# Two 16-wide attentions of a four-layer kernel: order of the first loads, place of the row statistics, and VectorE work ordered behind the maxima

## The chip, the cores and the metric

The kernel runs on one core of a Trainium2 chip. Its time is the device time of one execution in microseconds (us), the median of several runs. Engines are named as in the profile: PE (TensorE, with PEld for its weight loads), DVE (VectorE), ACT (ScalarE), POOL (GpSimd), SP (SyncE, which issues nearly all DMA transfers here). SBUF is the on-chip memory, PSUM the memory with eight banks that TensorE writes into.

## The reference

x has 16 batches of 256 rows and 256 columns, all float32, and ctx has the same shape. Four layers follow one another, each `x = x + attention(layernorm(x), ctx, ctx)` and `x = x + ffn(layernorm(x))`. The change is in the attentions of layers 0 and 3, which both have 16 heads that are 16 wide:

```
q = xn @ Wq.T (+ bq);  k = ctx @ Wk.T (+ bk);  v = ctx @ Wv.T (+ bv)     # split into 16 heads of 16
attn = softmax(q k^T / 4, over the 256 context rows)
x = x + (attn v, heads joined) @ Wo.T (+ bo)
```

Layer 0 has the biases, layer 3 has none (and shares keys and values in a way that its packed weights take care of). The feed-forward of layer 0 is quantized: the weights are rounded to -1, 0, 1 after a division by their mean absolute value, and the rows of x to 8 bits by their largest absolute value. Layers 1 and 2 are an mLSTM and a 64-wide attention with feed-forwards of their own; layer 3 ends with a mixture of eight experts.

## The kernel before

x stays in SBUF for the whole kernel, one tile per batch (128 partitions x 2 row tiles x 256). `SPECS` says in which order the pieces of a weight pack lie, and `load_pack` issues one transfer for each piece in that order. At the start SP issues the 16 tiles of x, then the eight pieces of `w_l0a`, the three of `w_l0f` (1 MB each), and then the first contexts (`cT`). VectorE computes each batch's row statistics (`batch_stats`: per row tile a BATCH_NORM_STATS2 and a BATCH_NORM_AGGREGATE) as x arrives, and `inv_std` takes all 32 inverse standard deviations at once, by a square root on ACT and a reciprocal on VectorE. That root needs another activation table than the exponentials, so a table is loaded after it.

`narrow_attention` is called by layer 0 (L559) and layer 3 (L1602). It walks over halves: a batch has 16 heads in four quads, and a quad has two halves of two heads. Half i belongs to batch b = i // 8, h = i % 8. Two passes over the scores run at once, and the second is 7 halves later (`LAG`):

- the first pass makes scores with queries on the partitions (`s_ps`, three PSUM banks); VectorE takes their row maxima (`maxima`, L319, two instructions per half, into `top`). After two quads the maxima are turned by TensorE (`top_rows`, `top_ps`) and added into a spare row of q, so that the second pass yields scores minus maximum;
- the second pass makes the scores again with keys on the partitions (`t_ps`, two banks); ACT takes the exponential (`exps`, L347); `weigh` multiplies them with the values (`acc_ps`, one bank, L359), whose extra column of ones yields the sum of the softmax.

The matmuls of both passes alternate within a half (L444): s, t, s, t for the first row tile, and the same for the second.

Around these, each half has other steps for the batches before and after it. All of them use the same two PSUM banks, called "misc", in turn: in h0 `context` (the load of cT of the next batch) and `enter` (normalize), h1 `turn` (`xnT_ps`, copied by ACT to xT) and `top_rows`, h2 `project` q (`qk_ps`), h3 `rest_of` q, h4 `project` k, h5 `rest_of` k and `top_rows`, h7 `values` (`v_ps`). `project` makes a projection on TensorE and lets ACT read it once for the even heads; `rest_of` (L281) is two VectorE instructions that read the same bank again for the odd heads. For an older batch: h2 and h5 `divide` (`o_ps`, L377: four transposes, then VectorE's division), h3 and h7 `back` (`oT_ps`, copied by ACT to oT), h6 `leave` (`out_ps`, the addition to x, the statistics for the next norm, and in layer 0 `left`: four reductions for the rows' largest and smallest value, `l0top`, L536, and every fourth batch the quantization steps).

A caller can add steps by `beside`. In layer 0 it takes one step of the `weights` generator per half from batch 1 on: twelve reductions of the feed-forward weights (`l0tot`, L500), then their rounding. In layer 3 it holds steps of the quantized feed-forward of layer 2, which ends beside the attention: `down` in h3 (`d_ps`, L1510), `steps_of`, `roots` (inverse deviations by `rsqrt`: logarithm and exponential on ACT, five instructions on POOL), the normed output and the experts' gate.

The order of the instructions on an engine is that in which the program issues them, changed by a scheduler of the language, which can move an instruction ahead of others that it doesn't depend on; `tc.issue_after(x)` keeps all that is issued under it behind x. In the built program before, the twelve `l0tot` reductions stand ahead of the first half. `rest_of` k stands ahead of the maxima of h5 and `rest_of` q ahead of those of h3, and the `l0top` reductions ahead of the maxima of h7 and h0.

Of the kernel before, what the change touches and what calls it, by code (L numbers as in the profile page):

```python
# [9 lines left out]
F32 = mybir.dt.float32  # L10
BF16 = mybir.dt.bfloat16
I32 = mybir.dt.int32
AF = mybir.ActivationFunctionType
# [4 lines left out]
P = 128  # L18
# [7 lines left out]

SPECS = {
    "w_l0a": [
        ("wq", 128, (2, 256)), ("wk", 128, (2, 256)), ("bq", 128, (2,)), ("bk", 128, (2,)),
        ("wv", 128, (2, 256)), ("bv", 128, (256,)), ("wo", 128, (2, 256)), ("bo", 128, (256,)),  # L30
    ],
    "w_l0f": [("wg", 128, (2, 1024)), ("wu", 128, (2, 1024)), ("wd", 128, (8, 256))],
    "w_l1a": [("gk", 128, (6, 8)), ("gb", 128, (8,)), ("os", 128, (256,))],
# [24 lines left out]
def kernel(ctx: ExitStack, tc: tile.TileContext, a: dict, out: bass.AP):  # L58
# [19 lines left out]
    nc.gpsimd.memset(eps6, 1e-6)  # L78

    X = [xp.tile([P, 2, D], F32, name=f"x{b}") for b in range(B)]  # L80
    for b in range(B):
        nc.sync.dma_start(X[b], x_v[b])

    def pool(stack, name, bufs, space=None):
        kw = {} if space is None else {"space": space}
# [29 lines left out]
        for t in range(2):  # L115
            tile_stats(mv, 2 * b + t, X[b][:, t, :])

    root = []

    def inv_std(mv):  # L120
        r = stat.tile([P, NT], F32, tag="rstd", name="rstd")
        root[:] = [nc.scalar.activation(r, mv[:, :, 1], AF.Sqrt, bias=eps5)]
        nc.vector.reciprocal(r, r)
        return r

    def normalize(dst, src, mv, r, i):
        nc.vector.tensor_scalar(dst, src, mv[:, i, 0:1], r[:, i : i + 1], ALU.subtract, ALU.mult)

# [8 lines left out]
                nc.tensor.transpose(pt[:, c, t * P : (t + 1) * P], xn[:, t, c * P : (c + 1) * P], ident)  # L137
        nc.scalar.copy(dst[:, :, dst_off : dst_off + S], pt)

    mv = new_stats()  # L140
    for b in range(B):
        batch_stats(mv, b)

    def bcast_max(col, wk, ps):

        t1 = ps.tile([1, P], F32, tag="misc", name="gm_ps")
# [7 lines left out]
        return m  # L154


    def narrow_attention(tag, w, mv, q_bias=None, k_bias=None, v_bias=None, add_bias=None,
                         new=None, rstd=None, wk=None, ps=None, before=None, between=None, beside=None, left=None, one_set=False):

        SCALE = 0.25
        with ExitStack() as st:
            one = pool(st, f"{tag}one", 1)
            if rstd is None:
                new = new_stats()
                rstd = inv_std(mv)
                if one_set:
                    with tc.issue_after(root[0].ins):
                        tables = nc.scalar.preload_act_table_set("natural_log_exp_and_others")  # L170
                    st.enter_context(tc.issue_after(tables.ins))
                wk = pool(st, f"{tag}wk", 2)
                ps = pool(st, f"{tag}ps", 2, PSUM)


            i32 = ident.rearrange("p (a b) -> p a b", b=32)
# [29 lines left out]
                nc.gpsimd.memset(t, 0.0)  # L206
            for t in vals:
                nc.gpsimd.memset(t[:, :, :, 16:17], 1.0)
            if v_bias is not None:

                bT = one.tile([P, 2, P], F32, name="bT")
                pb = ps.tile([P, 2, P], F32, tag="misc", name="bT_ps")
                for c in range(2):
                    nc.tensor.transpose(pb[:, c, :], v_bias[:, c * P : (c + 1) * P], ident)
                nc.vector.tensor_copy(bT, pb)
                pb = ps.tile([P, D], F32, tag="misc", name="bo_ps")
                for c in range(2):
                    nc.tensor.matmul(pb, lhsT=bT[:, c, :], rhs=w["wo"][:, c, :], start=(c == 0), stop=(c == 1))
                nc.vector.tensor_tensor(add_bias, pb, add_bias, ALU.add)

            state = {}

            def context(b):
                cT = wk.tile([P, 2, S], F32, tag="cT", name="cT", bufs=3)
                nc.sync.dma_start(cT, ctxT_v[b])
                state[b] = dict(cT=cT, v=vals[b % 3])

            def enter(b):

                xn = wk.tile([P, 2, D], F32, tag="xn", name="xn", bufs=3)  # L230
                for t in range(2):
                    normalize(xn[:, t, :], X[b][:, t, :], mv, rstd, 2 * b + t)
                if add_bias is not None:
                    for t in range(2):
                        nc.gpsimd.tensor_tensor(X[b][:, t, :], X[b][:, t, :], add_bias, ALU.add)
                state[b]["xn"] = xn

            def turn(b):
                s = state[b]
# [42 lines left out]

            def values(b):
                s = state[b]
                pv = ps.tile([P, 2, D], F32, tag="misc", name="v_ps")
                for t in range(2):
                    for c in range(2):
                        nc.tensor.matmul(  # L288
                            pv[:, t, :],
                            lhsT=s["cT"][:, c, t * P : (t + 1) * P],  # L290
                            rhs=w["wv"][:, c, :],
                            start=(c == 0),
                            stop=(c == 1),
                        )
# [19 lines left out]
            def maxima(n, made):  # L314
                par = n % 2
                top = tops[(n // 2) % 2]
                for j, sp, _ in made:
                    col = 32 * j + 16 - 16 * par
                    nc.vector.tensor_reduce(top[:, :, col], sp, AX.X, ALU.max)  # L319

            def top_rows(m):

# [77 lines left out]
            def leave(b):  # L400
                s = state.pop(b)
                po = ps.tile([P, 2, D], F32, tag="misc", name="out_ps")
                for t in range(2):
                    for c in range(2):
                        nc.tensor.matmul(  # L405
                            po[:, t, :],
                            lhsT=s["oT"][:, c, t * P : (t + 1) * P],
                            rhs=w["wo"][:, c, :],
                            start=(c == 0),
                            stop=(c == 1),  # L410
                        )
                nc.vector.tensor_tensor(X[b], po, X[b], ALU.add)
                batch_stats(new, b)
                if left is not None:
                    left(b, new)

            context(0)
            values(0)
            project(0, "k")
            rest_of(0, "k")  # L420
# [3 lines left out]
            turn(0)  # L424
            project(0, "q")
            rest_of(0, "q")
            if between is not None:
                between()

            LAG = 7  # L430
            halves = 8 * B
            for i in range(halves + (16 if beside is None else 40)):
                b, h = divmod(i, 8)
# [10 lines left out]
                        nc.tensor.matmul(out_, lhsT=l_, rhs=r_, start=True, stop=True)  # L444
                if made:
                    maxima(i // 2, made)
                if h == 5 and b + 1 < B:
                    rest_of(b + 1, "k")
                if flipped:
                    exps((i - LAG) // 2, flipped)  # L450
                if h % 4 == 1 and 5 <= i <= halves + 1:
# [4 lines left out]
                if b + 1 < B:  # L456
                    if h == 0:
                        context(b + 1)
                        enter(b + 1)
                    elif h == 1:  # L460
                        turn(b + 1)
                    elif h == 2:
                        project(b + 1, "q")
                    elif h == 3:
                        rest_of(b + 1, "q")
                    elif h == 4:
                        project(b + 1, "k")
                    elif h == 7:
                        values(b + 1)
# [12 lines left out]
        return new  # L482


    def l0_attn(mv, w, w_f, qp, load):
# [8 lines left out]

        def weights(ps):

            tot = qp.tile([P, 3, 4], F32, name="l0tot")
            for j, n in enumerate(names):
                for c in range(4):
# [24 lines left out]
        def beside(b, h, ps):  # L524
            if not made:
                made.append(weights(ps))
            if h == 4 and 8 <= b < 11:
                load(("w_l1a", "w_l1f", "w_l2a")[b - 8])
            if b >= 1:
                next(made[0], None)  # L530

        def left(b, new):

            for t in range(2):
                for j, op in enumerate((ALU.max, ALU.min)):
                    nc.vector.tensor_reduce(q["top"][:, 2 * b + t, j : j + 1], X[b][:, t, :], AX.X, op)  # L536
            if b % 4 < 3:
                return
            sl = slice(2 * b - 6, 2 * b + 2)
            mean = new[:, sl, 0]  # L540
            r = qp.tile([P, 8], F32, name=f"l0r{b}")
# [14 lines left out]

        with ExitStack() as st:
            sp = pool(st, "l0sp", 2)
            mv = narrow_attention(  # L559
                "l0a", w, mv, q_bias=w["bq"], k_bias=w["bk"], v_bias=w["bv"], add_bias=w["bo"], beside=beside, left=left,  # L560
                one_set=True,
            )
            for _ in made[0]:
                pass
        return mv, q
# [1372 lines left out]
    with ExitStack() as st:  # L1938
        keep = pool(st, "l3keep", 1)
        dram = pool(st, "l3dram", 1, bass.MemoryType.DRAM)  # L1940
        with ExitStack() as s2:
            qp = pool(s2, "l2fq", 1)
            with ExitStack() as s1:
                pw, packs = pool(s1, "l12w", 1), {}
                with ExitStack() as s0:
                    pq, pf, pa = pool(s0, "l0fq", 1), pool(s0, "l0fw", 1), pool(s0, "l0aw", 1)
                    wa = load_pack(pa, "w_l0a")
                    wf = load_pack(pf, "w_l0f")
                    mv, q0 = l0_attn(mv, wa, wf, pq, lambda n: packs.update({n: load_pack(pw, n, lambda z: not late(z))}))
# [116 lines left out]
```

## Time and profile before

| | |
|---|---|
| time of three runs | 3077.2, 3075.54, 3073.31 us, median 3075.54 |
| profiled execution | 3080.25 us, span 3078.5 us |
| layer 0's attention | first scores at 38.69 us, first turned batch after that (`xnT_ps`) at 67.8, then 91.7, 125.8, 152.7, 178.2; from there about 25.8 us a batch, up to 410.9 |
| layer 3's attention | about 2005 to 2452 us, 27.6 us a batch |
| mean granted TensorE clock | 0.951 |

Times in the profile are microseconds from the span's start. A timeline row is start, length, engine, line, operation, output<-input, shapes, how many instructions in a row, and in brackets the engine's idle time ahead of it with what ended that. Rows of the windows have the busy time of each engine in a stretch, with the number of instructions.

### The profile page before, as it was taken

The page shows a single profiled execution, that of the slowest core. Times are in us where ns is not written, and L with a number is a line of the kernel's source. Part 1 is how long each engine was busy: PE and PEld are TensorE (multiplying, and loading weights), DVE is VectorE, ACT ScalarE, POOL GpSimd, SP SyncE. Part 2 cuts the span into 40 slices and gives each one's busy share as a digit, 9 for nine tenths or more (in the row PEclk, how much of TensorE's full clock was granted, in tenths as well). Part 3 has the DMA queues.
Part 4 walks back from the last instruction along what each step waited for, and adds up shares of the span by engine and source line. Part 5 has one row for each costly group of instructions (what it writes and reads, how often), then busy time and mean ns, then how long its engine had stood idle before and what let it go on. Part 6 is the DMA issues. An engine that isn't in the chain of part 4 may idle for free.

```text
span 3078.5 us, 49357 instructions
## 1 busy us (share of the span) xinstructions
PE 2797.2 (91%) x18663; PEld 1990.1 (65%) x18683; DVE 1746.3 (57%) x4397; ACT 1256.5 (41%) x3267; POOL 966.1 (31%) x1929
## 2 busy tenths in 40 slices
PE   6999997778899999999999998698999959999996
PEld 4566664445666666666666665265666648888885
DVE  6777667944555555555555565987777661222221
ACT  2455556623444444444444444634555531111110
POOL 1100003334444444344433333311110034455552
PEclk9999999967999999999999999889999979999998
DMA  5000000010000000000000000411110035676774
GB/s 180 12 12 12 8 1 1 1 48 11 11 11 11 11 11 11 11 11 11 11 11 4 13 18 29 154 45 59 32 32 29 22 110 166 204 222 205 217 211 119
DMA packets 81771, 177.09 MB, mean 58 GB/s; under 512 B 25935, under 2 KB 50526, under 8 KB 70590
## 3 DMA queue, kind: packets, MB, share of 16 engines
q0 software_dynamic: 24864, 105.69, 11.4%
q1 hardware_dynamic: 56670, 68.25, 7.1%
q8 instruction: 147, 2.41, 0.3%
q14 instruction: 90, 0.74, 0.1%
HBM read 147.04 MB, written 31.06 MB: 58 GB/s over the span
## 4 chain that ended last, share of the span: by engine, by line
PE 73%; DVE 12%; POOL 5%; ACT 4%; issue 4%; DMA 1%; POOLq 0%; SPq 0%; DVEq 0%; ACTq 0%
PE h_ps L1857 8%; PE o_ps L1879 8%; PE s_ps L444 7%; PE qk_ps L1031 5%; PE acc_ps L359 4%; PE qk_ps L259 4%; PE acc_ps L1170 4%; PE out_ps L1091 4%; PE s_ps L1112 3%; PE eT_ps L1154 3%; PE v_ps L1047 2%; PE t_ps L444 2%; PE v_ps L288 2%; PE out_ps L405 2%; DVE low L1121 1%
## 5 line engine op out<-in xcount | busy, mean ns | idle before, releaser
L347 ACT ACTIVATE e<-t_ps 128x512 f32<-128x512 f32 x512 | 278.0, 594 | 229.4 <-PE t_ps L444 208.0
L319 DVE TENSOR_REDUCE top<-s_ps 128x2 f32<-128x512 f32 x512 | 330.9, 682 | 51.1 <-PE t_ps L444 44.5
L1131 ACT ACTIVATE e<-s_ps,low 128x256 f32<-128x256 f32 x512 | 236.2, 472 | 286.7 <-DVE low L1121 286.2
L444 PE MATMUL t_ps<-q,k 32*128 32x256 f32 x2048 | 336.2, 409 | 2.7 <-ACT e L347 2.6
L444 PE MATMUL s_ps<-k,q 32*128 32x256 f32 x2048 | 330.9, 411 | 8.4 <-DVE top L319 8.2
L1142 POOL TENSOR_SCALAR e<-e,total 128x256 f32<-128x256 f32 x512 | 238.5, 485 | 310.5 <-DVE total L1139 222.1
L1857 PE MATMUL h_ps<-xgT,w 128*128 128x256 f32 (+1 forms) x1248 | 254.6, 362 | 0.0
L1879 PE MATMUL o_ps<-w,h 128*128 128x256 f32 x1136 | 251.6, 379 | 0.0
L444 PEld LDWEIGHTS s_ps<-k,q 32*128 32x128 f32 x2048 | 197.3, 187 | 80.2 <-issue 35.4
L1857 PEld LDWEIGHTS h_ps<-xgT,w 128*128 128x128 f32 x1248 | 222.1, 192 | 27.6 <-ACT xgT L1846 0.2
L1121 DVE TENSOR_REDUCE low<-s_ps 128x2 f32<-128x512 f32 x256 | 164.3, 683 | 128.6 <-PE s_ps L1112 128.6
L1879 PEld LDWEIGHTS o_ps<-w,h 128*128 128x128 f32 x1136 | 212.9, 190 | 27.4
L444 PEld LDWEIGHTS t_ps<-q,k 32*128 32x128 f32 x2048 | 205.6, 187 | 20.3 <-ACT e L347 14.0
L1869 ACT ACTIVATE h<-h_ps,w 128x256 f32<-128x256 f32 (+1 forms) x156 | 62.5, 451 | 371.0 <-PE h_ps L1857 361.8
L1170 PE MATMUL acc_ps<-eT,v 128*64 128x256 f32 x1024 | 172.6, 397 | 42.3 <-DVE eT L1157 42.1
L1157 DVE COPY eT<-eT_ps 128x512 f32<-128x512 f32 x256 | 165.4, 678 | 21.2 <-PE eT_ps L1154 20.7
L1867 DVE TENSOR_SCALAR h<-h_ps,w 128x256 f32<-128x256 f32 (+1 forms) x156 | 64.6, 455 | 179.1 <-PE h_ps L1857 121.6
L1889 DVE TENSOR_TENSOR y<-o_ps,w 128x256 f32<-128x256 f32 x71 | 27.1, 420 | 226.3 <-PE o_ps L1879 226.3
L1170 PEld LDWEIGHTS acc_ps<-eT,v 128*64 128x64 f32 x1024 | 70.9, 136 | 128.3 <-DVE eT L1157 71.5
L1112 PE MATMUL s_ps<-k,q 64*128 64x256 f32 x1024 | 146.9, 403 | 0.1
L1154 PE MATMUL eT_ps<-ident,e 128*128 128x128 f32 x1024 | 143.9, 286 | 0.0
L359 PE MATMUL acc_ps<-e,vals 128*32 128x256 f32 x2048 | 142.6, 391 | 0.0
(476 smaller groups left out, 5579.3 us busy)
## 6 DMA issues: line engine op xcount, KB each, us to landing
cT<-in_ctxT_dram SPq DMA_DIRECT2D x32, 256.0 KB, 2.8
away<-h SPq DMA_DIRECT2D x30, 256.0 KB, 2.0
h<-away SPq DMA_DIRECT2D x30, 256.0 KB, 4.2
x<-in_x_dram SPq DMA_DIRECT2D x16, 256.0 KB, 5.9
w_l2a<-in_w_l2a_dram SPq DMA_DIRECT2D x4, 1024.0 KB, 6.5
c2T<-in_ctxT_dram SPq DMA_DIRECT2D x16, 256.0 KB, 2.7
c1T<-in_ctxT_dram SPq DMA_DIRECT2D x16, 256.0 KB, 2.7
va<-in_ctx_dram SPq DMA_DIRECT2D x32, 128.0 KB, 2.9
```

The lines of the kernel that those rows point to most:

```text
L319: nc.vector.tensor_reduce(top[:, :, col], sp, AX.X, ALU.max)
L347: nc.scalar.activation(e, tp, AF.Exp)
L359: nc.tensor.matmul(acc[32 * j : 32 * j + 32, par, :], lhsT=s["v"][:, k, 4 * g + j, 16 * par : 16 * par + 32], rhs=es[j][:, k, :], start=(k ...
L444: nc.tensor.matmul(out_, lhsT=l_, rhs=r_, start=True, stop=True)
L1112: nc.tensor.matmul(sp[j][:, t, :], lhsT=q[rows, g % 2, t * P : (t + 1) * P], rhs=k[rows, g % 2, :], start=True, stop=True,)
L1121: nc.vector.tensor_reduce(low[:, :, j], sp[j], AX.X, ALU.max, negate=True)
L1131: nc.scalar.activation(es[j][:, t, :], sp[j][:, t, :], AF.Exp, bias=low[:, t, j : j + 1], accum_out=total[:, t, j : j + 1])
L1142: nc.gpsimd.tensor_scalar(es[j][:, t, :], es[j][:, t, :], total[:, t, j : j + 1], 1.0, ALU.mult, ALU.mult)
L1154: nc.tensor.transpose(pt[:, k, t * P : (t + 1) * P], es[j][:, t, k * P : (k + 1) * P], ident)
L1170: nc.tensor.matmul(s["acc"][64 * j : 64 * j + 64, g % 2, :], lhsT=s["v"][g // 4][:, k, (2 * (g % 4) + j) * 64 : (2 * (g % 4) + j + 1) * 64 ...
L1857: nc.tensor.matmul(pp[:, f - f0, cols_], lhsT=w1[:, c * 1024 + f * P : c * 1024 + (f + 1) * P], rhs=xT[:, c, cols_], start=(c == 0), stop= ...
L1879: nc.tensor.matmul(pp[:, j, :], lhsT=h[:, f, j * P : (j + 1) * P], rhs=w2[:, f * D : (f + 1) * D], start=(f == 0), stop=(f == 7),)
```

## The change

- `w_l0a` is packed in another order: wv, wk, bk, wq, bq, bv, wo, bo. SP's queue starts with x of batch 0, cT of batch 0, these eight pieces, then x of batches 1 to 15 and the next cT. `w_l0f` is loaded by the `weights` generator, whose first step is taken in h7 of batch 0.
- `inv_std` is gone. `roots` uses `rsqrt` (logarithm and exponential) in five pieces: batches 0, 1, 2 to 3, 4 to 9 and 10 to 15. Only the statistics of batches 0 and 1 are computed before the first half; those of batch i + 2 are issued in half i.
- The fold of the value bias into the output bias (`bT`, `bo_ps`) comes after the projections of batch 0.
- `rest_of` k (h5), `rest_of` q (h3), those statistics and roots, and the `l0top` reductions and steps of layer 0 are issued under `tc.issue_after` of the half's last maximum. The reductions are put on a list (`due`) from which each half takes one entry.

In the built program after, VectorE has the two maxima of h3 ahead of `rest_of` q, the two of h5 ahead of `rest_of` k, and the `l0top` reductions two by two behind the maxima of h7 and h0; `l0tot` stands within halves 5 to 11. TensorE has the first three score matmuls of h6 (s, t, s) ahead of the four `o_ps` transposes of h5. In layer 3 `d_ps` has the bank that `oT_ps` had just before, and not that of `qk_ps`.

```diff
 SPECS = {
     "w_l0a": [
-        ("wq", 128, (2, 256)), ("wk", 128, (2, 256)), ("bq", 128, (2,)), ("bk", 128, (2,)),
-        ("wv", 128, (2, 256)), ("bv", 128, (256,)), ("wo", 128, (2, 256)), ("bo", 128, (256,)),
+        ("wv", 128, (2, 256)), ("wk", 128, (2, 256)), ("bk", 128, (2,)), ("wq", 128, (2, 256)), ("bq", 128, (2,)),
+        ("bv", 128, (256,)), ("wo", 128, (2, 256)), ("bo", 128, (256,)),
...
-    for b in range(B):
+
+    def load_x(b):
         nc.sync.dma_start(X[b], x_v[b])
+
+    load_x(0)
...
-    def inv_std(mv):
-        r = stat.tile([P, NT], F32, tag="rstd", name="rstd")
-        root[:] = [nc.scalar.activation(r, mv[:, :, 1], AF.Sqrt, bias=eps5)]
-        nc.vector.reciprocal(r, r)
-        return r
...
-    mv = new_stats()
-    for b in range(B):
-        batch_stats(mv, b)
...
+            def roots(lo, hi):
+                cols = slice(2 * lo, 2 * hi)
+                rsqrt(wk, rstd[:, cols], mv[:, cols, 1], ALU.add, 1.0, 1e-5)
+
+            context(0)
+            if fresh:
+                w = w()
+                q_bias, k_bias, v_bias, add_bias = (w[n] for n in ("bq", "bk", "bv", "bo"))
+                for b in range(1, B):
+                    load_x(b)
+                batch_stats(mv, 0)
+                roots(0, 1)
...
-                    nc.vector.tensor_reduce(top[:, :, col], sp, AX.X, ALU.max)
+                    last_max[:] = [nc.vector.tensor_reduce(top[:, :, col], sp, AX.X, ALU.max)]
...
                 batch_stats(new, b)
                 if left is not None:
-                    left(b, new)
-
-            context(0)
+                    due.extend(left(b, new))
+
             values(0)
...
+            biased(0)
+            if fresh:
+                batch_stats(mv, 1)
+                roots(1, 2)
...
-                if h == 5 and b + 1 < B:
-                    rest_of(b + 1, "k")
+
+                with tc.issue_after(last_max[0].ins):
+                    if h == 5 and b + 1 < B:
+                        rest_of(b + 1, "k")
+                    if h == 3 and b + 1 < B:
+                        rest_of(b + 1, "q")
+                    if fresh and i + 2 < B:
+                        batch_stats(mv, i + 2)
+                        for lo, hi in ((2, 4), (4, 10), (10, B)):
+                            if i + 3 == hi:
+                                roots(lo, hi)
+                    if due:
+                        due.pop(0)()
...
-                    elif h == 3:
-                        rest_of(b + 1, "q")
...
         def weights(ps):
 
+            w_f.update(load("w_l0f"))
+            yield
             tot = qp.tile([P, 3, 4], F32, name="l0tot")
...
-            if b >= 1:
+            if b >= 1 or h == 7:
                 next(made[0], None)
 
         def left(b, new):
 
-            for t in range(2):
+            def extremes(t):
                 for j, op in enumerate((ALU.max, ALU.min)):
                     nc.vector.tensor_reduce(q["top"][:, 2 * b + t, j : j + 1], X[b][:, t, :], AX.X, op)
-            if b % 4 < 3:
-                return
+
+            more = [lambda: extremes(0), lambda: extremes(1)]
+            return more + [lambda: steps(b, new)] if b % 4 == 3 else more
```

More of the change, by code (lines that the diff above doesn't have):

```diff
@@ L116, in batch_stats @@
             tile_stats(mv, 2 * b + t, X[b][:, t, :])
-    root = []
-    def inv_std(mv):
-        r = stat.tile([P, NT], F32, tag="rstd", name="rstd")
-        root[:] = [nc.scalar.activation(r, mv[:, :, 1], AF.Sqrt, bias=eps5)]
-        nc.vector.reciprocal(r, r)
-        return r
     def normalize(dst, src, mv, r, i):
@@ L154, in bcast_max, with narrow_attention @@
         return m
-    def narrow_attention(tag, w, mv, q_bias=None, k_bias=None, v_bias=None, add_bias=None,
-                         new=None, rstd=None, wk=None, ps=None, before=None, between=None, beside=None, left=None, one_set=False):
+    def narrow_attention(tag, w, mv, new=None, rstd=None, wk=None, ps=None, before=None, between=None, beside=None, left=None):
         SCALE = 0.25
@@ L164, in narrow_attention, with context @@
             one = pool(st, f"{tag}one", 1)
[L165 to L171, printed above, removed]
+            q_bias = k_bias = v_bias = add_bias = None
+            fresh, state = rstd is None, {}
+            if fresh:
+                new, mv = new_stats(), new_stats()
+                rstd = stat.tile([P, NT], F32, tag="rstd", name="rstd")
+                tables = nc.scalar.preload_act_table_set("natural_log_exp_and_others")
+                st.enter_context(tc.issue_after(tables.ins))
                 wk = pool(st, f"{tag}wk", 2)
                 ps = pool(st, f"{tag}ps", 2, PSUM)
+            def context(b):
+                cT = wk.tile([P, 2, S], F32, tag="cT", name="cT", bufs=3)
+                nc.sync.dma_start(cT, ctxT_v[b])
+                state[b] = dict(cT=cT)
+            def roots(lo, hi):
[9 more added lines that the diff above has]
+                roots(0, 1)
             i32 = ident.rearrange("p (a b) -> p a b", b=32)
@@ L208, in narrow_attention @@
                 nc.gpsimd.memset(t[:, :, :, 16:17], 1.0)
[L209 to L226, printed above, removed]
             def enter(b):
@@ L232, in enter, with biased @@
                     normalize(xn[:, t, :], X[b][:, t, :], mv, rstd, 2 * b + t)
+                if b:
+                    biased(b)
+                state[b]["xn"] = xn
+            def biased(b):
                 if add_bias is not None:
@@ L235, in enter @@
                         nc.gpsimd.tensor_tensor(X[b][:, t, :], X[b][:, t, :], add_bias, ALU.add)
-                state[b]["xn"] = xn
             def turn(b):
@@ L284, in values @@
                 s = state[b]
+                s["v"] = vals[b % 3]
                 pv = ps.tile([P, 2, D], F32, tag="misc", name="v_ps")
@@ L426, in narrow_attention @@
             rest_of(0, "q")
+            if v_bias is not None:
+                bT = one.tile([P, 2, P], F32, name="bT")
+                pb = ps.tile([P, 2, P], F32, tag="misc", name="bT_ps")
+                for c in range(2):
+                    nc.tensor.transpose(pb[:, c, :], v_bias[:, c * P : (c + 1) * P], ident)
+                nc.vector.tensor_copy(bT, pb)
+                pb = ps.tile([P, D], F32, tag="misc", name="bo_ps")
+                for c in range(2):
+                    nc.tensor.matmul(pb, lhsT=bT[:, c, :], rhs=w["wo"][:, c, :], start=(c == 0), stop=(c == 1))
+                nc.vector.tensor_tensor(add_bias, pb, add_bias, ALU.add)
+            biased(0)
+            if fresh:
+                batch_stats(mv, 1)
+                roots(1, 2)
             if between is not None:
@@ L430, in narrow_attention @@
             LAG = 7
+            last_max, due = [], []
             halves = 8 * B
@@ L482, in narrow_attention, with l0_attn @@
         return new
-    def l0_attn(mv, w, w_f, qp, load):
+    def l0_attn(w, w_f, qp, load):
         q = dict(
@@ L528, in beside, with steps @@
                 load(("w_l1a", "w_l1f", "w_l2a")[b - 8])
-            if b >= 1:
+            if b >= 1 or h == 7:
                 next(made[0], None)
         def left(b, new):
-            for t in range(2):
+            def extremes(t):
                 for j, op in enumerate((ALU.max, ALU.min)):
                     nc.vector.tensor_reduce(q["top"][:, 2 * b + t, j : j + 1], X[b][:, t, :], AX.X, op)
-            if b % 4 < 3:
-                return
+            more = [lambda: extremes(0), lambda: extremes(1)]
+            return more + [lambda: steps(b, new)] if b % 4 == 3 else more
+        def steps(b, new):
             sl = slice(2 * b - 6, 2 * b + 2)
@@ L558, in l0_attn @@
             sp = pool(st, "l0sp", 2)
[L559 to L562, printed above, removed]
+            mv = narrow_attention("l0a", w, None, beside=beside, left=left)
             for _ in made[0]:
@@ L1946, with load @@
                     pq, pf, pa = pool(s0, "l0fq", 1), pool(s0, "l0fw", 1), pool(s0, "l0aw", 1)
-                    wa = load_pack(pa, "w_l0a")
-                    wf = load_pack(pf, "w_l0f")
-                    mv, q0 = l0_attn(mv, wa, wf, pq, lambda n: packs.update({n: load_pack(pw, n, lambda z: not late(z))}))
+                    def load(n):
+                        if n == "w_l0f":
+                            return load_pack(pf, n)
+                        packs[n] = load_pack(pw, n, lambda z: not late(z))
+                    mv, q0 = l0_attn(lambda: load_pack(pa, "w_l0a"), {}, pq, load)
                     mv = l0_ffn(q0)
```

## The prediction

> **What bounds the kernel now.** I read the page's busy shares first, then the windows of the two 16-wide attentions, the groups of L319 and L444, the chain and the timeline of the start, and last the timeline of one batch in each attention.
>
> ```profile
> PE 2797.2 (91%) x18663; PEld 1990.1 (65%) x18683; DVE 1746.3 (57%) x4397; ACT 1256.5 (41%) x3267; POOL 966.1 (31%) x1929
> L319 DVE TENSOR_REDUCE top<-s_ps 128x2 f32<-128x512 f32 x512 | 330.9, 682 | 51.1 <-PE t_ps L444 44.5
> L444 PE MATMUL s_ps<-k,q 32*128 32x256 f32 x2048 | 330.9, 411 | 8.4 <-DVE top L319 8.2
> ```
> ```profile
> 40.00:68.00 28.00, 25.45 (x124) 16.91 (x124) 15.05 (x27) 5.90 (x12) 0.52 (x1) 0.76 0.23 89
> 68.00:92.00 24.00, 22.75 (x235) 14.68 (x236) 14.95 (x31) 13.59 (x30) 1.52 (x2) 1.00 0.05 13
> 92.00:126.00 34.00, 28.57 (x243) 17.95 (x244) 29.12 (x71) 14.03 (x30) 9.85 (x14) 0.89 0.03 9
> 153.00:410.00 257.00, 250.01 (x2432) 166.56 (x2434) 180.88 (x434) 137.74 (x295) 19.62 (x52) 1.00 0.04 10
> ```
> The windows' columns are stretch, length, then busy time of PE, PEld, DVE, ACT and POOL, granted clock, DMA share, GB/s. In layer 0's steady stretch (153 to 410) TensorE is busy 97%, so a wait that opens in its queue adds to the time, and a wait that closes can give back at most the 7 us that are left there. VectorE is 30% idle, and the 8.2 us that score matmuls wait for maxima in the whole kernel cap what earlier maxima can bring directly. Where VectorE is nearly full (92 to 126) the batch takes 34 us, not 25.8.
>
> The start, from the timeline:
> ```profile
> 0.80 9.87 SPq L82 DMA_DIRECT2D x<-in_x_dram  x16
> 11.07 5.58 SPq L97 DMA_DIRECT2D w_l0a<-in_w_l0a_dram  x8
> 17.00 1.50 SPq L97 DMA_DIRECT2D w_l0f<-in_w_l0f_dram  x3
> 18.55 1.68 SPq L225 DMA_DIRECT2D cT<-in_ctxT_dram  x3
> 24.65 7.20 DVE L500 TENSOR_REDUCE l0tot<-w_l0f 128x1 f32<-128x512 f32 x12
> 28.66 3.75 PE L288 MATMUL v_ps<-w_l0a,cT 128*128 128x256 f32 x8 [4.39 <-issue]
> 38.69 1.16 PE L444 MATMUL s_ps<-k,q 32*128 32x256 f32 x12 [0.22 <-ACT q L271]
> ```
> The first context, cT, is the 28th transfer issued, and v_ps starts only at 28.66. One half h5 of layer 0, then one h3 of layer 3:
> ```profile
> 242.90 0.99 DVE L281 TENSOR_SCALAR k<-qk_ps,mask,kadd 128x256 f32<-128x256 f32 x2 [3.10 <-ACT k L271]
> 243.81 1.28 DVE L319 TENSOR_REDUCE top<-s_ps 128x2 f32<-128x512 f32 x2
> 243.94 0.66 PE L377 MATMUL o_ps<-ident,o 128*128 128x128 f32 x4 [0.70 <-DVE k L281]
> 245.00 0.86 DVE L329 SCALAR_TENSOR_TENSOR q<-top_ps,spare,q 128x256 f32<-128x256 f32 x2
> 245.61 1.07 PE L359 MATMUL acc_ps<-e,vals 128*32 128x256 f32 x16
> ...
> 250.51 1.04 DVE L536 TENSOR_REDUCE l0top<-x 128x1 f32<-128x256 f32 x3
> ```
> ```profile
> 2251.99 1.80 PE L1510 MATMUL d_ps<-l2d,hq 128*128 128x256 bf16 x12 [0.29 <-DVE q L281]
> 2252.43 0.38 ACT L398 COPY oT<-oT_ps 128x256 f32<-128x256 f32 x1
> ```
> The o_ps transposes use the PSUM bank that held qk_ps of k, so they wait for VectorE's second read of it, and o_ps stands in TensorE's queue ahead of later scores.
>
> **The change, part by part**, against the profiled execution: 3080.25 us, span 3078.5, 0.15% above the median 3075.54. Negative is faster.
>
> *A, the start: -20.* The order becomes x0, cT, eight pieces of w_l0a (wv first), x1 to x15, cT, w_l0f. wv is then the third transfer; of the x tiles the second landed at 6.6 and the third's statistics ran at 7.36, so v_ps starts near 7.4. From v_ps to the first score took 38.69 - 28.66 = 10.03. Two short ACT steps for the inverse roots now stand ahead of the xT copy (about 0.5, by the 0.38 copy), and the bias fold (bo_ps, 2.08 for four matmuls at 22.20) comes between, about 1.0 of it uncovered: 18.9. The other path is x1, whose statistics VectorE runs before xn of batch 0: eleventh of SP's queue, issued near 7.4 at the x tiles' 0.6 us apart, landing after 2.9 (x0) to 5.9 (the page's median), then 0.75 of statistics, 0.73 of xn, 1.5 to 2 of turning and 4.4 from projecting q: 17.6 to 20.6 with the first steps partly beside it. Gain 18 to 22. POOL's new root steps stand ahead of its 2.6 us of memsets (1.52 to 4.1), which nothing needs before v_ps ends. w_l0f moves behind x15 and cT; its first reader comes in half 5 or later, and the cT behind it only a batch later: zero, and a late reduction would hold up VectorE's queue (rival 2).
>
> *B, VectorE work carried into batches 0 and 1: +4.* Statistics of 14 batches at 0.78 (two tiles at 0.39 from start to start) are 10.9, the twelve w_l0f reductions at 0.60 are 7.2: 18.1 us against the 22.0 that VectorE was idle in 40 to 92 (52.0 - 15.05 - 14.95). They fit, but unevenly. Nothing is one end; 8.5 for one batch that becomes as long as 92 to 126 is the other; I take 4, as neither window is yet full. The extra root steps on ACT (10 for 2) and POOL (25 more) lie beside PE: 0, and at most 1.7 with no cover (ten short steps at the 0.17 of mv, L112).
>
> *C, layer 0: +10.4.* The second read of k moves behind the two maxima of h5. Score matmuls of h5 start at T = 241.73. Where nothing stands ahead, maxima follow scores by 1.16 (scores 254.27, maximum 255.43): 242.89; the read comes 1.19 later (243.81 to 245.00) at 244.08, and o_ps 1.04 after it (242.90 to 243.94): 245.12 instead of 243.94. In the changed program's order three score matmuls of h6 (s, t, s) are issued ahead of o_ps, so they cover part of the wait; a t and the four of the second round are left. With o_ps 0.59 and, at worst, a whole half's 1.08 for these five, acc_ps starts at 246.76 against 245.61: +1.15, in 14 batches +16.1. If the five need only half the time, +0.6 each, +8.4. The other way, the four l0top reductions leave the front of h7's and h0's maxima: h0's scores took 1.52 (251.75 to 253.27) where a clean half takes 1.08; in the 13 batches that have both, 13 x -0.44 = -5.7 (0 if another wait is next: h4, at 262.53, takes 2.02 behind ACT). Moving the read of q behind h3's maxima delays no TensorE step of layer 0: oT_ps there is in the other bank. 16.1 - 5.7 = 10.4.
>
> *D, layer 3: +27.6.* Its o_ps waits in the same way. From the end of qk_ps of k (2257.72) to acc_ps took 3.73; by C's 5.03 from the start of h5 it is +1.3, x14 = 18.2; +0.75 each by C's lower case. In h3, d_ps now shares its bank with oT_ps and waits for the ACT copy, which ended at 2252.81, where d_ps started at 2251.99. Two score matmuls of h4 pass ahead, the other half-round and 1.07 follow d_ps: h4's scores end 4.38 after h3 instead of 3.53: +0.85, in 11 batches +9.4 (0 if they cover it all).
>
> Sum: -20 + 4 + 10.4 + 27.6 = +22.0, so 3102 for an execution like the profiled one, 3097.5 against the median. Ends: A -22, B 0, C 8.4 - 5.7 = 2.7, D 10.5 + 0 = 10.5 give -8.8 (3067); A -18, B 8.5 + 1.7, C 16.1, D 27.6 give +36 (3111).
>
> [...] In 44 to 64 TensorE was busy 3.0 to 4.0 of every 4 us, yet the granted clock was 0.68, 0.75, 0.82, 0.60, 0.54, and eight projection matmuls took 3.56 (60.45) against 1.99 warm (239.81). [...] I go by the row: the low clock comes along.
>
> **Rivals.**
> 1. *The other side: the waits stay covered.* If score matmuls that are issued ahead fill the later o_ps and d_ps, as the 7 us of total TensorE idle in 257 suggests that such gaps get filled, C and D keep only the gain: -20 + 4 - 5.7 = -21.7, 3054. It decides from 21.7 us over 39 waits (14 + 14 + 11): below 0.56 us each the change is no slower. Against it: o_ps already waits 0.70 with its reader first in VectorE's queue.
> 2. *VectorE fills in batches 0 and 1.* Were both to lengthen by 8.5 as batch 2 did, because w_l0f lands late or statistics wait for x behind maxima: B = 17, sum +35, 3110. For it, the row 92 to 126; against it, 22.0 of idle for 18.1.
> 3. *Only layer 0 shows it.* If the steps beside layer 3's attention leave TensorE spare (347 of 363 busy, 16 us idle in 13 batches), D is 0: -20 + 4 + 10.4 = -5.6, 3070.
>
> **How the numbers follow.** Chances: forecast 0.62, rival 1 0.10, rival 2 0.16, rival 3 0.12. The likeliest's own range is 3086 to 3108; the range 3066 to 3112 takes in rivals 2 and 3 and the ends of the sum, and leaves out rival 1 and the tails. About 0.2% (6 us) is what a measurement can tell from no change: faster by more (below 3069), rival 1 and nearly half of rival 3, 0.15; within (to 3082), the rest of rival 3 and the forecast's low tail, 0.10; slower 0.75.
>
> **What would show it.** A: the first s_ps near 19, not 38.7. B: batches 0 and 1 (first score to the third xnT_ps) near 57, not 53. C: VectorE's maxima of h5 ahead of k's read, o_ps idle on DVE k above 1, scores to acc_ps 5.0 instead of 3.88, h0's scores at 1.08, batch period 26.5 instead of 25.8. D: d_ps waiting for ACT oT, period 29.7 instead of 27.6. The prediction is wrong if o_ps waits no longer than 0.7, or if the earlier maxima free s_ps for halves that I counted as filled.

## The result and the profile after

The changed kernel takes 3116.72 us (median of four executions, 3109.18 to 3118.08) against 3076.37 for the kernel before: ratio 1.0126, 95% interval 1.0112 to 1.0141. In a later comparison (e1 below) it was 3108.21, ratio 1.0109 (1.0092 to 1.0126). Its eight executions lie in two groups, near 3108 and near 3117, and both profiled ones are of the lower group, so that the profiles show some 30 us of the loss, and where the other 8 lie is not seen. The forecast was 3097.5, within 3066 to 3112: the first median lies 5 us above that range, the second inside it.

The chain of the start first, in the timeline of the changed kernel:

```profile
6.37 3.75 PE L282 MATMUL v_ps<-w_l0a,cT 128*128 128x256 f32 x8 [6.37 <-DMA w_l0a<-in_w_l0a_dram]
14.16 1.99 PE L252 MATMUL qk_ps<-xT,w_l0a 128*128 128x256 f32 x8 [1.47 <-ACT xT L239]
16.80 0.69 PE L453 MATMUL s_ps<-k,q 32*128 32x256 f32 x2 [0.44 <-ACT q L264]
```

v_ps starts at 6.37 instead of 28.66, and the first scores at 16.80 instead of 38.69: 21.9 us gained. Next, the half h5 of layer 0, and h3 of layer 3, in the places that the prediction showed:

```profile
238.64 0.99 DVE L274 TENSOR_SCALAR k<-qk_ps,mask,kadd 128x256 f32<-128x256 f32 x2
239.54 0.86 DVE L323 SCALAR_TENSOR_TENSOR q<-top_ps,spare,q 128x256 f32<-128x256 f32 x2
239.68 0.66 PE L371 MATMUL o_ps<-ident,o 128*128 128x128 f32 x4 [0.80 <-DVE k L274]
241.32 1.07 PE L353 MATMUL acc_ps<-e,vals 128*32 128x256 f32 x16
```
```profile
2231.36 0.38 ACT L392 COPY oT<-oT_ps 128x256 f32<-128x256 f32 x1
2231.79 1.78 PE L1530 MATMUL d_ps<-l2d,hq 128*128 128x256 bf16 x12
2234.57 1.07 PE L353 MATMUL acc_ps<-e,vals 128*32 128x256 f32 x16
```

The scores of that h5 started at T = 236.27. o_ps stands at T + 3.41 and acc_ps at T + 5.05 (2.21 and 3.88 before). In layer 3, d_ps starts 1.59 after oT_ps, which follows h3's scores (2230.20; 0.72 before), behind the copy by ACT.

The groups of the page, to be held against L319 and L444 of before: VectorE is idle 111.7 us ahead of the maxima instead of 51.1, because scores come later. The scores are busy 350.1 us instead of 330.9 for the same 2048, though one of them takes 415 ns instead of 411. Matmuls that overlap count once in the busy time, so the group's time grows when a wait parts the matmuls of a half, as o_ps does with h6's: 1.17 and 1.12 us in two parts, where a whole half has 1.15. This growth alone is therefore no sign of a lower clock; in e10, below, with layer 0 at full clock, the group still has 344.5.

```profile
L313 DVE TENSOR_REDUCE top<-s_ps 128x2 f32<-128x512 f32 x512 | 331.1, 682 | 111.7 <-PE t_ps L453 97.9
L453 PE MATMUL s_ps<-k,q 32*128 32x256 f32 x2048 | 350.1, 415 | 16.5 <-DVE top L313 16.1
```

The windows by stage show where the time goes. Their columns are stretch, length, busy time (instructions) of PE, PEld, DVE, ACT, POOL, then the granted clock, DMA share and GB/s. The stages are bounded by the first score, the xnT_ps transposes of batch 4 and batch 15 of layer 0, and those of batch 1 and batch 15 of layer 3. Before:

```profile
38.70:125.80 87.10, 77.73 (x608) 50.08 (x609) 60.22 (x130) 34.19 (x71) 12.88 (x18) 0.88 0.11 42
125.80:410.60 284.80, 277.11 (x2687) 184.37 (x2686) 199.54 (x478) 151.86 (x325) 21.12 (x54) 1.00 0.04 10
410.60:2014.90 1604.30, 1449.42 (x8473) 975.23 (x8491) 975.83 (x2501) 737.98 (x2100) 600.78 (x1404) 0.94 0.07 20
2014.90:2409.30 394.40, 376.08 (x3556) 252.16 (x3555) 292.98 (x695) 188.94 (x423) 42.43 (x160) 0.96 0.12 36
```

After:

```profile
16.80:114.40 97.60, 84.02 (x616) 54.34 (x617) 81.36 (x204) 35.29 (x77) 21.69 (x41) 0.85 0.28 99
114.40:412.00 297.60, 288.86 (x2685) 189.94 (x2685) 200.50 (x475) 152.25 (x325) 20.04 (x49) 0.98 0.04 9
412.00:2009.50 1597.50, 1443.14 (x8472) 969.38 (x8491) 976.08 (x2504) 736.95 (x2100) 599.42 (x1409) 0.95 0.07 20
2009.50:2436.60 427.10, 409.91 (x3555) 269.28 (x3555) 293.21 (x695) 191.41 (x423) 42.23 (x160) 0.95 0.11 34
```

| stage | before | after | difference |
|---|---|---|---|
| start to the first score | 38.7 | 16.8 | -21.9 |
| batches up to the turn of batch 4 | 87.1 | 97.6 | +10.5 |
| layer 0 from there | 284.8 | 297.6 | +12.8 |
| end of layer 0 to the start of layer 3 | 1604.3 | 1597.5 | -6.8 |
| layer 3 | 394.4 | 427.1 | +32.7 |
| the rest | 669.2 | 670.9 | +1.7 |

The sum is +29.0, the difference of the spans (3107.5 and 3078.5). TensorE's share of busy time in layer 0 is the same 97% before and after, and yet the stage is 12.8 us longer: 288.86 us busy instead of 277.11, with 2687 and 2685 instructions. Part of that is the parted halves, and part the granted clock, which fell from 1.00 to 0.98. The loss by the clock is estimated here as (1 - clock) x busy time, summed over the windows of 5 us that lie whole in a stage, from one multiple of 5 to the next: 0.0 us before in layer 0's stage and 5.6 after, 12.3 before and 20.4 after in layer 3's, 63.3 and 55.2 in the unchanged stage between. The first 4 us of layer 0's stage before, which these windows leave out, lost 1.3 more. That unchanged stage took 1593 to 1604 us in the profiles of all kernels here, so a profile's span by itself is worth some 10 us either way, and the stages are what to compare.

### The profile page after: what moved, and what is told of

It reads as the page before. It is cut to its first block, busy times and chain, and to the rows that moved or that the text cites. A ratio compares the mean times of both kernels' runs of the same rounds, so it can differ in the third digit from the quotient of the medians.

```text
span 3107.5 us, 49353 instructions
## 1 busy us (share of the span) xinstructions
PE 2841.3 (91%) x18662; PEld 2010.3 (65%) x18683; DVE 1750.0 (56%) x4396; ACT 1258.3 (40%) x3275; POOL 967.3 (31%) x1954
## 4 chain that ended last, share of the span: by engine, by line
PE 74%; DVE 12%; POOL 5%; ACT 4%; issue 3%; DMA 1%; SPq 0%; POOLq 0%; DVEq 0%; ACTq 0%
PE h_ps L1877 8%; PE o_ps L1899 8%; PE s_ps L453 6%; PE qk_ps L1051 5%; PE acc_ps L353 4%; PE acc_ps L1190 4%; PE qk_ps L252 4%; PE t_ps L453 4%; PE out_ps L1111 4%; PE s_ps L1132 3%; PE eT_ps L1174 3%; PE v_ps L1067 2%; PE out_ps L399 2%; PE v_ps L282 2%; DVE top L313 2%
## 5 line engine op out<-in xcount | busy, mean ns | idle before, releaser
L313 DVE TENSOR_REDUCE top<-s_ps 128x2 f32<-128x512 f32 x512 | 331.1, 682 | 111.7 <-PE t_ps L453 97.9
L453 PE MATMUL s_ps<-k,q 32*128 32x256 f32 x2048 | 350.1, 415 | 16.5 <-DVE top L313 16.1
L453 PE MATMUL t_ps<-q,k 32*128 32x256 f32 x2048 | 358.9, 411 | 4.4 <-ACT e L341 4.2
L453 PEld LDWEIGHTS t_ps<-q,k 32*128 32x128 f32 x2048 | 214.7, 187 | 36.8 <-ACT e L341 23.6
L1190 PE MATMUL acc_ps<-eT,v 128*64 128x256 f32 x1024 | 172.2, 397 | 41.7 <-DVE eT L1177 41.6
L353 PE MATMUL acc_ps<-e,vals 128*32 128x256 f32 x2048 | 148.9, 405 | 0.0
```

The source lines that it names most:

```text
L313: last_max[:] = [nc.vector.tensor_reduce(top[:, :, col], sp, AX.X, ALU.max)]
L353: nc.tensor.matmul(acc[32 * j : 32 * j + 32, par, :], lhsT=s["v"][:, k, 4 * g + j, 16 * par : 16 * par + 32], rhs=es[j][:, k, :], start=(k ...
L1190: nc.tensor.matmul(s["acc"][64 * j : 64 * j + 64, g % 2, :], lhsT=s["v"][g // 4][:, k, (2 * (g % 4) + j) * 64 : (2 * (g % 4) + j + 1) * 64 ...
```

## The experiments

Two theories were put up first. Theory 1: the reads of k and q that moved behind the maxima hold up o_ps and d_ps, and through them TensorE's queue, by the times in the prediction. Theory 2: VectorE is full in the first batches, and the low clock has causes of its own. After the first four runs the question became why the moved read cost more than the waits (theories A and B).

**e1: the changed kernel again**

> The changed kernel as it is, for a second profile beside the first (3109.18 us, three other executions 3116 to 3118). Theory 1 (the moved reads of k and q hold o_ps and d_ps up): the period of a batch is again 26.5 us in layer 0 and 29.8 us in layer 3, first scores at 16.8 us, and what differs between executions lies in layers 1 and 2 as stretches at a low granted clock; 3112 to 3118. Theory 2 (VectorE full in the first batches, and more low clock in the attentions because of the waits): the periods themselves spread, and the attentions take several us more in a slower execution.

Measured: 3108.21 us (3107.58 to 3115.93), span 3106.1. The periods of the batches (from one xnT_ps to the next) were the same batch for batch: 26.5 us in layer 0's steady stretch with 28.1 in the same place, 29.8 in layer 3 with 31.4 and 33.1 in the same two places (33.0 in the first profile). The expectation gave the loss at a low clock to layers 1 and 2; the runs show it in the attentions too, and repeated there, so the program makes it. Of layer 0's stretch 8.6 us were lost to the clock this time, of layer 3's 20.1.

**e2: the read of k free again**

```diff
-                with tc.issue_after(last_max[0].ins):
-                    if h == 5 and b + 1 < B:
-                        rest_of(b + 1, "k")
+                if h == 5 and b + 1 < B:
+                    rest_of(b + 1, "k")
+                with tc.issue_after(last_max[0].ins):
```

> The changed kernel with VectorE's read of k in half 5 back ahead of the maxima; all else as changed. Theory 1: o_ps starts 1.15 us earlier in 14 batches of layer 0 and 1.3 in 14 of layer 3, so 16 + 18 = 34 us less than the changed kernel, about 3082; period 25.4 in layer 0, 28.5 in layer 3. Theory 2: nothing in the first batches or in the clock changes, so over 3105.

Measured: 3066.62 us, ratio to before 0.9965 (0.9953 to 0.9976), 41.6 us less than the changed kernel in the same comparison. The periods are 25.3 and 28.4 us, as expected. So the moved read of k alone turns a gain into the loss; theory 2 falls. But it gave back 8 us more than its waits.

**e3: both reads free**

The edit of e2, and:

```diff
-                    if h == 3 and b + 1 < B:
-                        rest_of(b + 1, "q")
...
+                    elif h == 3:
+                        rest_of(b + 1, "q")
```

> The changed kernel with both reads (k in half 5, q in half 3) at their old places; the order of the loads, the statistics in the halves and the l0top reductions behind the maxima remain. Theory 1: 34 us less for k and 11 x 0.85 = 9 for d_ps in layer 3, so about 3073, just below the kernel before; what is left is the start (-22), the fuller batches 0 and 1 (+10) and about -6 from the reductions, which would make 3058 if all three stood alone. Theory 2: over 3100.

Measured: 3054.93 us, ratio 0.9931 (0.9915 to 0.9948). This is 18 us less than the 3073 that was expected from the waits, and near the 3058 of the three parts. The period of layer 3 is back at 27.6. The medians of e2 and e3 differ by 11.7 us, where the wait behind the read of q was to be 9. But not all of that is its price: layer 3's stage took 398.9 us in e2's profile and 395.3 in e3's, and the unchanged stage before it was 7 us shorter in e3's. In layer 3's steady batches the read costs 0.8 us each (28.4 and 27.6), as the prediction had it (0.85).

**e4: the read of k behind the maxima, alone, in the kernel before**

```diff
...
-                if h == 5 and b + 1 < B:
-                    rest_of(b + 1, "k")
+                with tc.issue_after(last_max[0].ins):
+                    if h == 5 and b + 1 < B:
+                        rest_of(b + 1, "k")
```

> The kernel before with one thing of the change: the read of k in half 5 behind the half's maxima, in both layers. Theory 1: 14 x 1.15 + 14 x 1.3 = 34 us more than before, about 3110. Theory 2: the moved read costs little where VectorE isn't full, so within 8 us of before.

Measured: 3133.09 us, ratio 1.0183 (1.0166 to 1.02), 55.4 us more than before, where the waits make 34. One moved pair of VectorE instructions costs more than the whole change. By stage, layer 0 took 309.6 us instead of 284.8 and layer 3 425.2 instead of 394.4. In windows of e4: the two stages, then the 3.4 us around the wait in one batch's h5, and what followed:

```profile
126.10:435.70 309.60, 301.06 (x2686) 195.37 (x2685) 200.62 (x478) 153.41 (x325) 21.07 (x54) 0.95 0.03 9
2029.20:2454.40 425.20, 403.92 (x3554) 266.27 (x3555) 294.63 (x695) 190.33 (x423) 41.68 (x160) 0.93 0.11 34
...
252.80:256.20 3.40, 2.83 (x28) 1.36 (x20) 2.87 (x6) 1.58 (x4) 0.00 (x0) 1.00 0.01 2
256.50:263.30 6.80, 6.80 (x34) 3.77 (x26) 1.79 (x5) 1.57 (x3) 0.00 (x0) 0.50 0.00 0
```

The granted clock is 0.50 for 6.8 us right behind the o_ps of that half. Eight matmuls of out_ps, which take 1.99 us in the batch before, took 3.73 there.

**e5: the same with TensorE kept at work in the wait**

On e4's kernel:

```diff
-                for t in range(2):
-                    nc.tensor.transpose(pt[:, t * P : (t + 1) * P], tops[m % 2][:, t, :], ident)
+                for _ in range(4 if m % 2 == 0 else 1):
+                    for t in range(2):
+                        nc.tensor.transpose(pt[:, t * P : (t + 1) * P], tops[m % 2][:, t, :], ident)
```

> The kernel with the read of k alone pinned (3133.1 us), and each of the two transposes of top_ps in half 5 made four times instead of once: the wait of o_ps stays as long, but TensorE is idle for some 0.8 us less of it. Theory A (a TensorE that is idle for a large enough part of a short stretch gets a lower clock in the next): the low clock in layer 0's steady stretch goes from 11.5 us lost to under 2, layer 3 from 27 to under 15, and the time falls by 15 to 30 us to 3103 to 3118, though TensorE does more. Theory B (the low clock there comes from something else, as the phase or another engine): no fall, 3130 to 3140.

Measured: 3111.37 us, ratio 1.0118 (1.0101 to 1.0135), 21.7 us less than e4, though TensorE has 192 more transposes in the two attentions. Windows of e5, the stages as for e4:

```profile
127.40:426.30 298.90, 292.27 (x2753) 194.93 (x2752) 200.46 (x478) 153.08 (x325) 21.07 (x54) 0.99 0.03 9
2025.70:2439.10 413.40, 391.80 (x3638) 263.54 (x3639) 294.36 (x695) 190.12 (x423) 42.49 (x160) 0.97 0.11 35
```

The loss by the clock went from 11.5 to 1.2 us in layer 0's stage and from 27.2 to 8.9 in layer 3's. What is left over the kernel before is 14.1 and 19.0 us, 33 in all, near the waits as the prediction priced them (16.1 + 18.2). Theory B, which foresaw no fall, falls.

**e6: the l0top reductions behind the maxima, alone, in the kernel before**

```diff
...
-                    left(b, new)
+                    due.extend(left(b, new))
...
+                with tc.issue_after(last_max[0].ins):
+                    if due:
+                        due.pop(0)()
...
```

> The kernel before with one thing of the change: the l0top reductions two by two behind the maxima of later halves. Theory 1: h0's scores take 1.08 us instead of 1.52, period 25.3 instead of 25.75 in layer 0, 13 x 0.44 = 5.7 us less than before, about 3071. The rival that the next wait (ACT in half 4) takes it: 0.

Measured: 3070.13 us, ratio 0.998 (0.9971 to 0.999), 5.6 less than before; layer 0's period is 25.3. This term of the sum is right.

**e7: both reads behind the maxima, in layer 3 alone, in the kernel before**

```diff
...
-                if h == 5 and b + 1 < B:
+                if tag == "l0a" and h == 5 and b + 1 < B:
                     rest_of(b + 1, "k")
+                if tag == "l3a":
+                    with tc.issue_after(last_max[0].ins):
+                        if h == 5 and b + 1 < B:
+                            rest_of(b + 1, "k")
+                        if h == 3 and b + 1 < B:
+                            rest_of(b + 1, "q")
...
-                    elif h == 3:
+                    elif h == 3 and tag == "l0a":
                         rest_of(b + 1, "q")
```

> The kernel before with both reads (k in half 5, q in half 3) behind the maxima in layer 3 alone. By the waits alone 15 x (1.3 + 0.85) = 32 us, less the batches at the ends, so 27 to 32; by the profile of the changed kernel its layer 3 took 33 more, 8 of them at a lower clock; so about 3105 to 3111. If layer 3's cost came from anything else of the change: within 6 us of before.

Measured: 3110.38 us, ratio 1.0112 (1.0095 to 1.0129), +34.6. Its layer 3 took 426.8 us, with the periods of the changed kernel batch for batch (29.8, and 31.4 and 33.0 in the same places). Layer 3's loss is made by the two reads there and nothing else.

**e8: a version that beats both**

On e3's kernel, the reductions and the rounding of the feed-forward weights are spread over more batches, and each stands behind its half's maxima.

```diff
-            if b >= 1 or h == 7:
+            if b < 2:
+                if h == 7 and b == 0:
+                    next(made[0], None)
+            elif b < 4 or h % 2 == 0:
                 next(made[0], None)
...
-                    beside(b, h, ps)
+                    with ExitStack() as pinned:
+                        if fresh:
+                            pinned.enter_context(tc.issue_after(last_max[0].ins))
+                        beside(b, h, ps)
```

> The changed kernel with both reads at their old places (3054.9 us) and the weights' steps of layer 0 spread: the twelve reductions from batch 2 on, the rounding from batch 4 on in every second half, each behind the half's maxima. If VectorE's full stretch in batches 1 to 3 (28.6, 29.0 and 33.8 us instead of 25.4) is what is left of the loss, these fall to 25.5 to 27 and the time to 3041 to 3047; if it is the cold clock or the late statistics, within 4 us of 3055.

Measured: 3039.85 us (3038.58 to 3042.76), ratio 0.9886 (0.9869 to 0.9902): 35.9 us less than the kernel before and 15.1 less than e3, a little below the 3041 to 3047 expected. From batch 2's turn to batch 5's, periods of 26.3, 25.3 and 25.4 stand where e3 had 29.0, 33.8 and 26.7. On the page of e8 VectorE is idle only 41.0 us ahead of the maxima, where the kernel before had 51.1 and the changed one 111.7:

```profile
L313 DVE TENSOR_REDUCE top<-s_ps 128x2 f32<-128x512 f32 x512 | 330.0, 680 | 41.0 <-PE t_ps L453 33.0
```

**e9: the start alone**

On e3's kernel, the l0top reductions go back to their old place.

```diff
-                    due.extend(left(b, new))
+                    for z in left(b, new):
+                        z()
```

> The kernel before with the start alone: order of the loads, roots in pieces, statistics inside the halves (behind the maxima); both reads of k and q and the l0top reductions where they were. By difference (3054.9 for the kernel with both reads free, 5.6 less for the reductions alone) 3060 to 3061, 15 to 17 us less than before. If the start gains only together with the reductions, over 3066; the prediction's A and B would make it 16 less.

Measured: 3061.35 us, ratio 0.9955 (0.9938 to 0.9972), 15.0 less than before. By stage, batch 4 is turned at 113.7 instead of 125.8, 12.1 earlier, and from there to batch 15 both take 284.8.

**e10: the changed kernel with TensorE kept at work**

The edit of e5, in the changed kernel.

> The changed kernel with each of the two transposes of top_ps in half 5 made four times. Theory A (idle TensorE brings low clock): no low clock in layer 0's steady stretch, layer 3's loss from 20 us to under 12, so 12 to 16 us less than the changed kernel, 3095 to 3103, which is what the waits alone cost in the prediction. Theory B (the low clock has another cause): no fall, over 3108.

Measured: 3099.59 us, ratio 1.0075 (1.0058 to 1.0091). Windows of the two stages:

```profile
114.70:407.80 293.10, 286.37 (x2752) 191.93 (x2751) 201.01 (x476) 152.23 (x325) 20.03 (x49) 1.00 0.03 10
2007.30:2427.70 420.40, 401.38 (x3640) 269.07 (x3640) 293.55 (x695) 191.69 (x423) 42.23 (x160) 0.97 0.11 34
```

Layer 0's stage is 8.3 us and layer 3's 26.0 us over the kernel before, and the three batches with longer periods (28.1, 31.4, 33.0) are at 26.6 and 29.8. With the start (batch 4 at 114.7, 11.1 earlier) that makes -11.1 + 8.3 + 26.0 = +23.2, and the medians differ by the same (3099.59 - 3076.38). That both agree to a tenth, and come near the +22.0 of the prediction's sum, is partly luck: the two profiles differ by 19.2, as the unchanged stage was shorter in e10's, and the first batches are here some 10 us longer where the sum had 4.

## Why the prediction was wrong, point by point

The direction and the mechanism of the waits were right, and the size was off by 8 to 18 us: +30 to +40 measured for +22. Two terms were mis-sized: VectorE's work in the first batches, and the waits, which were priced at full clock. By the stages of the first profile, the misses are -1.9 us in A, +6.5 in B, +2.4 in C and +5.1 in D, with -5.1 in the stages that the change leaves alone; the first waits of C fall into B's stage.

- **A, the start (-20):** -21.9 to the first score, the upper end of the range, for two reasons. v_ps starts at 6.37 and not near 7.4, since the prediction misread a row: in the trace of before the statistics that waited until 6.6 were those of the third x tile, not of the second, so the third transfer could be expected at 6.6. And from v_ps to the first score it is 10.43 and not 11.5, since bo_ps comes at 17.43, behind the first scores.
- **B, VectorE's work in batches 0 and 1 (+4):** from the first score to the turn of batch 3 it is 62.7 us (16.80 to 79.48) instead of 52.7 (38.69 to 91.35): +10, as much as the upper bound (8.5, 10.2 with the roots), so rival 2 was half true. In windows: before, changed, e10.

```profile
38.70:91.30 52.60, 48.65 (x362) 31.80 (x363) 30.59 (x59) 19.66 (x41) 3.03 (x4) 0.87 0.17 64
16.80:79.50 62.70, 54.12 (x371) 35.37 (x372) 51.89 (x133) 21.00 (x47) 11.81 (x27) 0.84 0.42 149
17.20:80.20 63.00, 53.16 (x382) 34.63 (x383) 51.87 (x133) 21.02 (x47) 11.81 (x27) 0.89 0.40 146
```

VectorE has 21 us more to do there. The clock isn't what made the stretch longer: in e10 it is above that of before, and the stretch is 63.0. Nor are the moved reads and the l0top reductions, since e9, without them, has 62.3 (16.93 to 79.25). The step that failed is "they fit": idle time was counted over two whole batches, and that work put anywhere in them would find it free. e3 still takes 61.8 there (15.63 to 77.38), and e8 57.0 (16.47 to 73.5): with all but one of the weights' reductions out of the stretch, +4.3 is left for the statistics and the roots. The part that was priced too low was the weights' reductions. That they hurt because each stands between the maxima of one half is argued and not shown.
- **C, layer 0's waits (+10.4):** the steps were right to hundredths: o_ps at T + 3.41 for T + 3.39, acc_ps at T + 5.05 for T + 5.03, h0's scores at 1.08, period 26.5. With TensorE kept at work the stage costs 8.3 (e10). The change costs 12.8 in its first profile and some 16 in its second, because the waits also bring low clock: 5.6 and 8.6 us in the two, 0.0 before.
- **D, layer 3 (+27.6):** d_ps waits for ACT's copy, h4's scores end 4.37 after h3 (4.38), the period is 29.8 (29.7). With TensorE kept at work 26.0, in the changed kernel 32.7, of which 8.1 are the greater loss by the clock.

The other step that failed is the price of C and D: they were waits alone, at full clock, and the low clock that the waits bring stood at nothing, though the prediction let the low clock of the start come along. In the changed kernel it is 5.6 and 8.1 us. e4 and e5 measure it apart: the same wait cost 55 us with the low clock that it brought, and 36 where TensorE was given work in it. What the executions near 3117 have beyond those near 3108 stays open. The sign that was given for a false step, o_ps idle above 1 us on DVE k, was itself too coarse: the idle time right before o_ps is 0.80, since the three scores that pass ahead split it, and the whole delay is 1.2.

*Rival 1* (the waits stay covered) fell: every one of the 39 showed. In the changed kernel's profile all 28 o_ps start 1.04 or 1.05 us after the moved read, and all 11 d_ps 0.05 after ACT's copy. *Rival 2* held in part, as said. *Rival 3* (only layer 0 shows it) fell with e7: layer 3 is the larger part.

The prediction's choice to go by the row held: the early batches of the changed kernel ran at 0.85, against 0.88 before, so the low clock did come along with the earlier start. In e3 it even stayed at half for 23.8 us there, with TensorE recorded as busy throughout:

```profile
29.40:53.20 23.80, 23.80 (x117) 14.63 (x115) 20.33 (x53) 6.92 (x15) 1.27 (x6) 0.50 0.47 155
```

## What to carry to other kernels

Before an instruction is ordered behind another, look for who reuses its input's buffer: here two short VectorE reads held a PSUM bank, and the transposes that wanted the bank stood ahead of all later scores in TensorE's queue. Here a wait in the queue of TensorE, which was busy 97% in layer 0's stage, had its full price (33 us over both stages in e5, priced at 34.3), and a price on top where the granted clock fell behind it (55 us in e4, at 0.95 and 0.93 in the two stages, 1.00 and 0.96 before); so a forecast of such a wait needs a second bound, and the stage's clock has to be read beside its length. Where one edit has several parts, try them one by one: here two parts gain (15 and 6 us) and one loses more than both.

## What the runs showed of the hardware

Low clock came here behind stretches in which TensorE worked most of the time. In layer 0's steady stretch the clock of the changed kernel went to half (0.51 in the window) for 3.4 us, one stretch behind another of 3.4 us in which TensorE was busy 2.60 us, 0.77 of it. The wait of the next batch, with the same busy share, has full clock (1.00) behind it. Windows of the changed kernel:

```profile
290.60:294.00 3.40, 2.60 (x22) 1.69 (x20) 3.40 (x11) 0.98 (x2) 0.00 (x0) 1.00 0.02 5
294.00:297.40 3.40, 3.40 (x21) 1.55 (x20) 1.26 (x3) 1.47 (x3) 0.00 (x0) 0.51 0.00 0
...
318.00:321.40 3.40, 2.60 (x28) 1.52 (x20) 2.64 (x6) 1.81 (x4) 0.00 (x0) 1.00 0.01 2
321.40:324.80 3.40, 3.40 (x34) 2.17 (x33) 2.23 (x7) 1.46 (x3) 0.00 (x0) 1.00 0.02 5
```

Windows of 3.5 us, slid in steps of 0.25 over the steady stretches of both attentions (from 180 and from 2175 us to the last turn), have these least busy shares of TensorE, with the drops to half clock that start in the stretch:

| kernel | layer 0: least share, drops | layer 3: least share, drops |
|---|---|---|
| before | 0.80, none | 0.84, none |
| changed | 0.77, 1 | 0.77, 3 |
| e2 | not shown | 0.84, none |
| e3 | 0.80, none | 0.84, none |
| e4 | 0.77, 3 | 0.77, 1 |
| e5 | 0.83, none | 0.82, none |
| e6 | 0.80, none | 0.84, none |
| e7 | 0.80, none | 0.77, 3 |
| e8 | 0.80, none | 0.84, none |
| e9 | 0.80, none | 0.84, none |
| e10 | 0.82, none | 0.82, none |

Of the 11 drops 10 come right behind 3.41 us in which TensorE was busy 0.77, and one (e4, 256.5) behind 0.83, though the least share of e3's layer 0, without a drop, is 0.80. In the changed kernel o_ps waits 0.79 or 0.80 us in each of the 18 batches of its two stretches, and 4 drops follow: at 294.1 in layer 0, and at 2331.85, 2362.57 and 2424.01 in layer 3, which are 30.72 and 61.44 apart; in e7 the three have the same distances. What sets these few batches apart from the others with the same wait, and whether the phase that theory B named plays a part, no run here settles.

At the start of the kernel before, the values of 0.54 to 0.82 from 44 to 64 are means over full and half clock: it was half (0.50) from 43.16 to 46.57, from 49.99 to 53.40 and from 56.82 to 63.65, and full (1.00) between. TensorE was busy 0.72 and 0.65 of the windows of 3.41 us right ahead of the first two, which is no more than ahead of the drops above, but 0.93 of that ahead of the third. Why that one came, and why the clock stayed low so long in e3, no run here settles.
